# Last image of an attention layer: another order of its four head pairs, an output projection in two halves of the queries, and statistics read from the PSUM bank

## The chip, the cores and the metric

The kernel runs on one core of a Trainium2 chip. The metric is the device time of one execution in microseconds; the profile is of one execution, and its span lies a little under that execution's time.

## The reference

Four layers follow one another on x of shape 8 x 384 x 32 x 32, each added to its input. The change lies in the end of the first one, an attention over the 1024 pixels of each image with 8 heads of 48 channels:

```python
q = _dwproj(x, dw_q, g_q, b_q, pw_q).reshape(B, heads, hd, N)   # k and v alike
attn = softmax(einsum('bhcn,bhcm->bhnm', q, k) * scale)
out = einsum('bhnm,bhcm->bhcn', attn, v).reshape(B, C, H, W)
out = einsum('oc,bchw->bohw', w_out, out)
return _bn(out, g_out, b_out)      # mean and variance over all 8 images and all pixels
```

`_dwproj` is a depthwise 3x3 convolution, a batch normalisation, a GELU and a 384 x 384 projection. The second layer (a mixture of experts on the pixels, after a group normalisation of x plus this output) can't begin before the batch normalisation's statistics over all images are known. Layers three (a ternary convolution) and four (deformable attention) come after it.

## The kernel before

**Stages.** Stage A (until about 550 us) convolves all images and writes the raw results to memory. Stage B, where the change lies, is the attention, image after image (until about 1822 us). Then come `norms` (the batch normalisation's scale and shift, and the group statistics of what follows), a branch (L805) that recomputes the layer in a safer way if a softmax denominator was out of bounds, and the experts, which load their weights `w_sb` (L943) behind the branch.

**How stage B is tiled.** Channels lie on the 128 partitions, in KC = 3 blocks of 128; queries are cut into two halves of HALF = 512, keys into NT8 = 8 blocks of 128. The 8 heads are worked on as NPAIR0 = 4 pairs. Pairs 0, 1 and 2 carry 48 of each 64 rows of a block of projected queries and keys (`qk`); the rows that are left over in the three blocks make the two heads of pair 3. `gather_last` (L471, on SP's queue) copies them to `ql` as each block is projected. So pair 3 reads `ql` where the others read `qk`.

**Units and steps.** A unit is one pair with one half of the queries; it has four steps of NS = 2 key blocks. A step issues the scores (L638) of the step after it, the exponentials on ScalarE (L645), and then `weigh` (L653) of its own, which adds exp x values into two PSUM banks `pav`. At the second step of a unit (`kc == NS`) up to four entries of the list `todo` are issued as well: projections of the next pair (`project`, L572), projections of the output (`out_project`, L590), values. A scheduler keeps ScalarE in the order written and places the rest; TensorE runs its queue in order.

**`normalise`** (from L607) ends a unit on VectorE. It adds the two banks into `ta` (L610, L611), transposes blocks of 32 x 32 into `tu` (L614), where column HQ0 = 24 of each 32 holds the softmax denominator, takes its reciprocal into `rec` (L615), multiplies (L616) and transposes back. For pairs 0, 1 and 2 the result goes into channel block `pr` of `att` (L621). There 24 of each 32 rows are the pair's own and 8 belong to pair 3. For pair 3 it goes into `al` (L624), and `place_last` (L482) moves it as twelve strips of 8 rows x 512 (16 KB): strips 0 to 3 into block 0 of `att`, 4 to 7 into block 1, 8 to 11 into block 2. They are issued on SP, but for the very last unit alternately on SP and ScalarE's queue.

**`out_project`** multiplies `wo0` with the three blocks of `att` into a bank `po` (L590, three matmuls of 128x512). In the last image ScalarE copies the bank to `ot` (L601), VectorE takes `bn_stats` of `ot` (L602), ScalarE's queue stores `ot` (L603), and `cross` multiplies `ot` with the input half `xh` (L488; `xh` is loaded on SP, L587), sums it (L489) and aggregates (L141). `xh` and `ot` have two buffers each. `bank` takes from a pool of four PSUM banks that `pav` shares.

**End of the last image.** The units are in the order of pairs 0, 1, 2, 3. The output projection of queries 0 to 511 is queued in the second step of pair 3's second unit; that of queries 512 to 1023 follows the last unit. Then VectorE checks all of `rec` (L742, L743, L745), a matmul with ones (L747) and L748 make the flag `bad` of it, and `norms` begins: three aggregates over all images (L154), variance plus epsilon (L160), the power -0.5 on GpSimd (L95), the scale (L162) and a chain of small operations.

Of the kernel before, what the change touches and what calls it, by code (L numbers as in the profile page):

```python
# [9 lines left out]
ALU = mybir.AluOpType  # L10
AX = mybir.AxisListType

B, C, H, W = 8, 384, 32, 32
N = H * W
P = 128
KC = C // P
HALF = N // 2
# [8 lines left out]
NH0, HD0, NPAIR0 = 8, 48, 4  # L26
HQ0 = HD0 // 2
HS0 = 32 - HQ0
R_LO, R_HI = 1e-15, 1e15
# [23 lines left out]
def tile_kernel(ctx: ExitStack, tc: tile.TileContext, i: dict, out: bass.AP):  # L53
    nc = tc.nc
# [12 lines left out]
    def bank(name):  # L67
        return ps_mm.tile([P, HALF], F32, tag="mm", name=name)
# [148 lines left out]
    with ExitStack() as pa:  # L217
# [10 lines left out]
        for s in range(2):  # L228
            t = wa.tile([P, KC, H + 2, W], F32, name=f"pad{s}")
# [134 lines left out]
        for n, (b, g) in enumerate(work):  # L364
# [6 lines left out]
            if n in todo:  # L371
                f, b2 = todo.pop(n)
# [10 lines left out]
            for h, k in steps:  # L383
                dx, c0, c1, o0 = TAPS[k]
                rows = slice(h * (H // 2), (h + 1) * (H // 2))
                if g < NGC:
                    lhs, rhs = cw[:, g, dx, :], st[:, rows, c0:c1]
                else:
                    r = slice(32 * h, 32 * h + 3 * GR)
                    lhs, rhs = cwr[r, dx, :], st[r, rows, c0:c1]  # L390
                nc.tensor.matmul(  # L391
                    pk[h].rearrange("p (h w) -> p h w", w=W)[: 3 * nch, :, o0 : o0 + c1 - c0],
                    lhsT=lhs, rhs=rhs, start=(k == 0), stop=(k == 2),
                )
                if k == 2:
                    hs = slice(h * HALF, (h + 1) * HALF)
# [30 lines left out]
        for k, t in enumerate(two):  # L427
# [8 lines left out]
            start=True, stop=True,  # L436
# [3 lines left out]
            start=True, stop=True,  # L440
# [32 lines left out]
                in_=src[64 * j + HD0 : 64 * (j + 1), :],  # L473
            )

    def place_last(dst, src, queues):

        for k in range(12):
            j, d = divmod(8 * k, HD0)
            r = 64 * j + 32 * (d // HQ0) + d % HQ0  # L480
            q = 32 * (k % 4) + HQ0
            queues[k % len(queues)].dma_start(  # L482
                out=dst[q : q + HS0, k // 4, :], in_=src[r : r + HS0, :]
            )

    def cross(b, m, h, xh, ot):

        nc.vector.scalar_tensor_tensor(xh, xh, xmv[:, b, m, 0:1], ot, ALU.subtract, ALU.mult)  # L488
        nc.vector.reduce_sum(xo[:, b, m, h : h + 1], xh, AX.X)  # L489
        if h == 1:  # L490
            moments(omv[:, b, m, :], ost[:, m, 2 * b : 2 * b + 2, :])
# [11 lines left out]
    with ExitStack() as pb:  # L503
# [76 lines left out]
            if h == 1:  # L580
                gather_last(qks[b, KC, v], qks[b, pr, v], pr)

        def out_project(b, m, h):
            hs = slice(h * HALF, (h + 1) * HALF)
            xh = op.tile([P, HALF], F32, tag="xh", name=f"xh{b}_{m}_{h}")
            with tc.issue_after(w_last.ins) if b == 0 else nullcontext():
                nc.sync.dma_start(out=xh, in_=x_img[b][:, m, hs])  # L587
            po = bank(f"po{b}_{m}_{h}")
            for c in range(KC):
                nc.tensor.matmul(  # L590
                    po,
                    lhsT=wo0[:, c, m * P : (m + 1) * P],
                    rhs=atts[b][:, c, hs],
                    start=(c == 0),
                    stop=(c == KC - 1),
                )
            ot = op.tile([P, HALF], F32, tag="ot", name=f"ot{b}_{m}_{h}")
            if b + 1 < B:
                nc.vector.tensor_copy(ot, po)
            else:  # L600
                nc.scalar.copy(ot, po)  # L601
            nc.vector.bn_stats(ost[:, m, 2 * b + h, :], ot)  # L602
            (nc.sync if b + 1 < B else nc.scalar).dma_start(out=o_dram[b, :, m, hs], in_=ot)  # L603
            cross(b, m, h, xh, ot)

        def normalise(b, pr, h, pav):

            u = b * NU + pr * 2 + h
            ta = np_.tile([P, HALF], F32, tag="ta", name=f"ta{u}", bufs=1)
            nc.vector.tensor_copy(ta, pav[0])  # L610
            nc.vector.tensor_tensor(ta, pav[1], ta, ALU.add)  # L611
            tu = np_.tile([P, 16, 32], F32, tag="tu", name=f"tu{u}", bufs=1)
            tuf = tu.rearrange("p a b -> p (a b)")
            nc.vector.transpose(tuf, ta)  # L614
            nc.vector.reciprocal(rec[:, u, :], tu[:, :, HQ0])  # L615
            nc.vector.tensor_tensor(  # L616
                tu, tu, rec[:, u, :].unsqueeze(2).to_broadcast([P, 16, 32]), ALU.mult
            )
            hs = slice(h * HALF, (h + 1) * HALF)
            if pr < KC:  # L620
                nc.vector.transpose(atts[b][:, pr, hs], tuf)  # L621
            else:
                al = np_.tile([P, HALF], F32, tag="al", name=f"al{u}")
                nc.vector.transpose(al, tuf)  # L624
                last = b + 1 == B and h == 1
                place_last(
                    atts[b][:, :, hs], al, (nc.sync, nc.scalar) if last else (nc.sync,)
                )

        def scores(b, pr, h, kc):  # L630

# [16 lines left out]
        def weigh(b, pr, kc, pav, p):  # L648
            for k in range(2):
                r = slice(64 * k, 64 * k + 64)  # L650
                for j in range(2):
                    hd = 2 * pr + j
                    nc.tensor.matmul(  # L653
                        pav[k][64 * j : 64 * j + 64, :],
                        lhsT=vts[b % 2][r, kc, 2 * hd : 2 * hd + 2, :].rearrange(
                            "p a b -> p (a b)"
                        ),
                        rhs=p[r, j * HALF : (j + 1) * HALF],
                        start=(kc == 0),
                        stop=(kc == NT8 - 1),  # L660
                    )
# [4 lines left out]
        for v in range(2):  # L666
            for h in range(2):
                project(0, 0, v, h)

        NS = 2  # L670
        steps = [
            (b, pr, h, kc)
            for b in range(B) for pr in range(NPAIR0) for h in range(2)
            for kc in range(0, NT8, NS)
        ]
        todo = [lambda t=t: values(0, t) for t in range(NT8)]
# [8 lines left out]
        for n, (b, pr, h, kc) in enumerate(steps):  # L685
            if kc == 0:
                if pr == 0 and h == 0:
                    atts[b] = ap_.tile([P, KC, N], F32, tag="att", name=f"att{b}")
                    if b + 1 < B:
                        load_b(b + 1)  # L690
                    else:
                        for k in range(3):
                            fetch(k)
                if b == 0 and pr == 1 and h == 0:
                    values_tile(1)
                if b + 1 == B and pr == 2 and h == 0:
                    for k in range(3, 5):
                        fetch(k)
                if b + 1 == B and pr == 3 and h == 1:
                    todo += [lambda m=m: out_project(B - 1, m, 0) for m in range(KC)]  # L700
                if h == 0 and pr + 1 < KC:
                    todo += [
                        lambda v=v, q=q, b=b, pr=pr: project(b, pr + 1, v, q)
                        for v in (1, 0) for q in range(2)
                    ]
                if pr == 0 and h == 1 and b > 0:
                    todo += [
                        lambda m=m, q=q, b=b: out_project(b - 1, m, q)
                        for m in range(KC) for q in range(2)
                    ]  # L710
                if pr == 2 and h == 0 and b + 1 < B:
                    todo += [lambda t=t, b=b: values(b + 1, t) for t in range(NT8)]
                if pr == 3 and h == 0 and b + 1 < B:
                    todo += [
                        lambda v=v, q=q, b=b: project(b + 1, 0, v, q)
                        for v in (1, 0) for q in range(2)
                    ]
                pav = [bank(f"pav{b}_{pr}_{h}_{k}") for k in range(2)]
            cur = nxt
            if n + 1 < len(steps):  # L720
                nxt = scores_of(*steps[n + 1])
            if b + 1 < B:
                for v, c in GELUS.get(n % (len(steps) // B), ()):
                    gelu_chunk(acts[b + 1][2 - v], 2 - v, c)
            for k in range(NS):
                weigh(b, pr, kc + k, pav, cur[k])

            early = b == 0 and pr == 0 and h == 0
            if early or kc == NS:
                for _ in range(min(2 if early else 4, len(todo))):  # L730
                    todo.pop(0)()
            if kc == NT8 - NS:
                normalise(b, pr, h, pav)
        for t in todo:
            t()

        for m in range(KC):
            out_project(B - 1, m, 1)

        okt = pp.tile([P, B * NU * 16], F32, tag="p", name="okt")  # L740
        recf = rec.rearrange("p u q -> p (u q)")
        nc.vector.tensor_scalar(okt, recf, R_LO, None, ALU.is_ge)  # L742
        nc.vector.scalar_tensor_tensor(okt, recf, R_HI, okt, ALU.is_le, ALU.mult)  # L743
        okm = np_.tile([P, 1], F32, tag="okm", name="okm", bufs=1)
        nc.vector.tensor_reduce(okm, okt, AX.X, ALU.min)  # L745
# [59 lines left out]
    with tc.If(redo > 0):  # L805
        with ExitStack() as pb:
# [13 lines left out]
            with tc.For_i(0, B) as bi:  # L820
# [40 lines left out]
                for pr in range(NPAIR0):  # L861
                    qt, kt = qks[0][:, pr, :], qks[1][:, pr, :]
                    for h in range(2):
# [40 lines left out]
                                )  # L904
                        hs = slice(h * HALF, (h + 1) * HALF)
                        nc.vector.tensor_copy(att[:, pr, hs] if pr < KC else al[:, hs], pav)
                place_last(att, al, (nc.sync,))
                oe = work[4]
                for m in range(KC):
                    for h in range(2):  # L910
# [983 lines left out]
```

## Time and profile before

| | |
|---|---|
| median of 3 runs | 3751.69 us (3746.74 to 3756.45) |
| profiled execution, its own time | 3751.05 us |
| its span | 3749.3 us |
| mean granted TensorE clock | 0.981 |
| TensorE matmul busy | 3632.0 us (97%) |
| VectorE busy | 1820.6 us (49%) |
| ScalarE busy | 1280.2 us (34%) |
| a unit of the last image without projections | 13.75 us (1763.12 to 1776.87, `ta` to `ta`) |
| last weighing ends, branch is left | 1804.2 us, 1835.1 us |

A line of the timeline gives start, duration, engine, source line, operation, output <- input, count, and in brackets the idle time of the engine before it and what ended it. A float32 matmul has two records. "SPq" and "ACTq" are the queues that issue transfers, PE is TensorE, DVE VectorE, ACT ScalarE, POOL GpSimd. The table by windows has the window, its length, busy time and count of each engine, granted clock, share of the DMA engines and GB/s.

### The profile page before, as it was taken

What the parts mean: (1) busy time and instruction counts of PE and PEld (TensorE: products, weight loads), DVE (VectorE), ACT (ScalarE), POOL (GpSimd) and SP (SyncE); (2) the same over time, 40 slices, a digit from 0 to 9 for tenths busy, and PEclk for the clock granted to TensorE, in tenths of its full rate; (3) what the DMA queues carried; (4) which work ended last, traced back from release to release, by engine and by line L of the source; (5) the groups of instructions that cost most, each with busy time, mean ns of one, the idle gap of its engine ahead of it and who ended that gap; (6) DMA issues with size and microseconds to landing.
All of it is one profiled execution on the core that took longest, in us unless ns stands there. A gap on an engine that the chain in (4) does not pass through costs nothing.

```text
span 3749.3 us, 39325 instructions
## 1 busy us (share of the span) xinstructions
PE 3632.0 (97%) x15746; PEld 1533.0 (41%) x15746; DVE 1820.6 (49%) x2840; ACT 1280.2 (34%) x1536; POOL 199.5 (5%) x162
## 2 busy tenths in 40 slices
PE   7999999999999999999799999999999999999888
PEld 3444333333333333333244534444444444544433
DVE  6776223232323232333346557465663656547664
ACT  2222354545444454534112321323222232322222
POOL 0000100000000000000000010201001010010111
PEclk8999999999999999999899999999999999999898
DMA  6776311121212121211430000100001001010000
GB/s 198 232 251 229 131 54 36 62 63 37 63 40 75 26 72 28 71 43 55 183 140 34 17 34 17 40 28 17 34 17 51 17 17 40 19 43 17 0 34 18
DMA packets 83449, 242.49 MB, mean 65 GB/s; under 512 B 18563, under 2 KB 19091, under 8 KB 82873
## 3 DMA queue, kind: packets, MB, share of 16 engines
q1 hardware_dynamic: 70174, 200.42, 16.1%
q10 hardware_dynamic: 12504, 37.88, 3.0%
q8 instruction: 128, 2.10, 0.2%
q0 software_dynamic: 576, 1.55, 0.1%
q14 instruction: 67, 0.54, 0.0%
HBM read 122.64 MB, written 75.50 MB: 53 GB/s over the span
## 4 chain that ended last, share of the span: by engine, by line
PE 40%; DVE 9%; ACT 1%; issue 0%; DMA 0%; POOL 0%; DVEq 0%; POOLq 0%; ACTq 0%; SPq 0%
PE y L1281 11%; PE ph L1260 8%; DVE y L1355 6%; PE pq L1400 3%; PE pw L1363 3%; PE pf L1666 3%; PE s L1561 3%; PE pav L1577 2%; PE pss L1603 1%; DVE hd L1246 1%; DVE off L1470 1%; PE pk L1535 1%; PE pv L1544 1%; PE xsb L1521 1%; PE pom L1483 1%; PE plog L1023 0%
## 5 line engine op out<-in xcount | busy, mean ns | idle before, releaser
L645 ACT ACTIVATE p<-s 128x1024 f32<-128x1024 f32 x512 | 496.5, 1021 | 506.8 <-PE s L638 506.6
L1281 PE MATMUL y<-hd,w_sb 128*128 128x512 f32 x1080 | 490.2, 599 | 3.6 <-DVE hd L1246 3.6
L653 PE MATMUL pav<-p,vt 64*64 64x512 f32 x4096 | 487.0, 590 | 0.0
L1260 PE MATMUL ph<-h,w_sb 128*128 128x512 f32 x1104 | 483.3, 594 | 0.4 <-DMA w_sb<-in_w_dram 0.4
L638 PE MATMUL s<-qk,qk 48*64 48x512 f32 x3072 | 370.8, 597 | 3.3 <-ACT p L645 3.3
L391 PE MATMUL pk<-st,cw_sb 126*126 126x512 f32 x720 | 322.8, 610 | 9.5 <-DMA st<-pad 9.3
L1260 PEld LDWEIGHTS ph<-h,w_sb 128*128 128x128 f32 x1104 | 207.6, 190 | 253.5 <-issue 250.3
L1281 PEld LDWEIGHTS y<-hd,w_sb 128*128 128x128 f32 x1080 | 199.0, 191 | 249.3 <-issue 235.5
L653 PEld LDWEIGHTS pav<-p,vt 64*64 64x64 f32 x4096 | 156.6, 133 | 285.1 <-issue 285.1
L610 DVE COPY ta<-pav 128x512 f32<-128x512 f32 x64 | 44.2, 691 | 429.0 <-PE pav L653 425.9
L1355 DVE SCALAR_TENSOR_TENSOR y<-h,tap,y 128x992 f32<-128x992 f32 (+1 forms) x192 | 234.0, 1242 | 1.6
L391 PEld LDWEIGHTS pk<-st,cw_sb 126*126 126x126 f32 x720 | 140.4, 197 | 183.8 <-issue 179.1
L1470 DVE SCALAR_TENSOR_TENSOR off<-q,dw_sb,off 128x225 f32<-128x225 f32 (+3 forms) x432 | 213.1, 546 | 1.7
L1270 ACT ACTIVATE hd<-ph,b_sb 128x512 f32<-128x512 f32 x180 | 122.7, 681 | 258.6 <-PE ph L1260 258.3
L638 PEld LDWEIGHTS s<-qk,qk 48*64 48x64 f32 x3072 | 108.6, 133 | 231.1 <-issue 191.9
L78 DVE COPY qk<-pq 128x512 f32<-128x512 f32 x48 | 33.2, 691 | 292.7 <-PE pq L572 292.7
L397 ACT COPY y<-pk 126x512 f32<-126x512 f32 (+1 forms) x136 | 76.4, 583 | 255.2 <-PE pk L391 111.1
L1568 ACT ACTIVATE p<-s 128x1024 f32<-128x1024 f32 x96 | 93.1, 1021 | 173.0 <-PE s L1561 172.9
L590 PE MATMUL po<-att,wo_sb 128*128 128x512 f32 x288 | 132.8, 615 | 11.6 <-DMA att<-al 11.6
L1246 DVE TENSOR_TENSOR hd<-hd,cb 128x512 f32<-128x512 f32 x180 | 122.3, 684 | 35.5 <-ACT hd L1270 35.2
L1363 PE MATMUL pw<-y,upw 128*128 128x512 f32 x288 | 129.7, 603 | 7.6 <-DVE y L1355 7.6
L572 PE MATMUL pq<-g,wq_sb 128*128 128x512 f32 x288 | 131.2, 606 | 2.2 <-DMA wq_sb<-in_wq_dram 2.2
(280 smaller groups left out, 3961.2 us busy)
## 6 DMA issues: line engine op xcount, KB each, us to landing
g<-raw SPq DMA_DIRECT2D x72, 512.0 KB
st<-pad SPq DMA_DIRECT2D x180, 168.0 KB
raw<-y ACTq DMA_DIRECT2D x171, 168.0 KB
xa<-in_x_dram SPq DMA_DIRECT2D x24, 512.0 KB
xh<-in_x_dram SPq DMA_DIRECT2D x48, 256.0 KB
f<-in_x_dram SPq DMA_DIRECT2D x24, 512.0 KB
f<-o SPq DMA_DIRECT2D x24, 512.0 KB
o<-ot SPq DMA_DIRECT2D x42, 256.0 KB
```

The costliest lines, as they stand in the source:

```text
L391: nc.tensor.matmul(pk[h].rearrange("p (h w) -> p h w", w=W)[: 3 * nch, :, o0 : o0 + c1 - c0], lhsT=lhs, rhs=rhs, start=(k == 0), stop=(k = ...
L572: nc.tensor.matmul(pq, lhsT=w_in[v][:, c, pr * P : (pr + 1) * P], rhs=acts[b][v][:, c, h * HALF : (h + 1) * HALF], start=(c == 0), stop=(c ...
L590: nc.tensor.matmul(po, lhsT=wo0[:, c, m * P : (m + 1) * P], rhs=atts[b][:, c, hs], start=(c == 0), stop=(c == KC - 1),)
L638: nc.tensor.matmul(s[64 * k : 64 * k + 64, j * HALF : (j + 1) * HALF], lhsT=kt[r, k0 : k0 + 64], rhs=qt[r, h * HALF : (h + 1) * HALF], sta ...
L645: nc.scalar.activation(p, s, AF.Exp, scale=scale)
L653: nc.tensor.matmul(pav[k][64 * j : 64 * j + 64, :], lhsT=vts[b % 2][r, kc, 2 * hd : 2 * hd + 2, :].rearrange("p a b -> p (a b)"), rhs=p[r, ...
L1246: nc.vector.tensor_tensor(hd, hd, state["cb"], ALU.mult)
L1260: nc.tensor.matmul(ph, lhsT=w1[:, e, c, dc * P : (dc + 1) * P], rhs=state["h1"][c], start=(c == 0), stop=(c == KC - 1),)
L1281: nc.tensor.matmul(y, lhsT=w2[:, e, dc, m * P : (m + 1) * P], rhs=state[h, k], start=(k == 0), stop=(k == NE * KC - 1),)
L1355: nc.vector.scalar_tensor_tensor(d, f, tap2[:, c, t : t + 1], d, ALU.mult, ALU.add)
L1363: nc.tensor.matmul(pw[h], lhsT=upw2[:, c, m * P : (m + 1) * P], rhs=y[c][:, hs], start=(c == 0), stop=(c == KC - 1),)
L1470: nc.vector.scalar_tensor_tensor(d, f, dw3[:, t : t + 1], d, ALU.mult, ALU.add)
```

## The change

In the last image the order of the pairs is 0, 1, 3, 2. Pair 3's strips for channel blocks 0 and 1 of `att` go there as before, since those blocks are complete. Those for block 2 go to a spare place (`spare(0, h)`, in the values tile that the last image doesn't use), VectorE transposes that into `spare(1, h)`, and `normalise` of pair 2 writes its 24 of each 32 columns beside them there, so that one transpose writes the whole of block 2. All strips are issued on SP. `normalise` of the very last unit works by two halves of 256 queries, and so does the output projection behind it, into three banks that are taken beforehand. The statistics of that projection read the bank in place of `ot`. The check of `rec` is issued after the last transpose.

```diff
-    def place_last(dst, src, queues):
+    def place_last(dst, src, third=None):
         for k in range(12):
...
-            queues[k % len(queues)].dma_start(
-                out=dst[q : q + HS0, k // 4, :], in_=src[r : r + HS0, :]
-            )
+            to = dst[:, k // 4, :] if k < 8 or third is None else third
+            nc.sync.dma_start(out=to[q : q + HS0, :], in_=src[r : r + HS0, :])
...
-        def out_project(b, m, h):
+        def out_project(b, m, h, po=None):
...
-            po = bank(f"po{b}_{m}_{h}")
-            for c in range(KC):
+            po_new = po is None
+            if po_new:
+                po = bank(f"po{b}_{m}_{h}")
+            for c in range(KC if po_new else 0):
...
-            nc.vector.bn_stats(ost[:, m, 2 * b + h, :], ot)
+            nc.vector.bn_stats(ost[:, m, 2 * b + h, :], ot if po_new else po)
...
+        def spare(k, h):
+            vf = vts[B % 2].rearrange("p t h d -> p (t h d)")
+            return vf[:, (2 * k + h) * HALF : (2 * k + h + 1) * HALF]
...
         def normalise(b, pr, h, pav):
...
+            tv, tf = tu, tuf
+            if b + 1 == B and pr == 2:
+                tf = spare(1, h)
+                tv = tf.rearrange("p (a b) -> p a b", b=32)[:, :, :HQ0]
+            n = 2 if b + 1 == B and pr == 2 and h == 1 else 1
+            for k in range(n):
+                qs, qb = (slice(k * m // n, (k + 1) * m // n) for m in (HALF, 16))
+                nc.vector.tensor_copy(ta[:, qs], pav[0][:, qs])
+                nc.vector.tensor_tensor(ta[:, qs], pav[1][:, qs], ta[:, qs], ALU.add)
+                nc.vector.transpose(tuf[:, qs], ta[:, qs])
+                nc.vector.reciprocal(rec[:, u, qb], tu[:, qb, HQ0])
+                w = tv.shape[2]
+                nc.vector.tensor_tensor(
+                    tv[:, qb], tu[:, qb, :w],
+                    rec[:, u, qb].unsqueeze(2).to_broadcast([P, 16 // n, w]), ALU.mult,
+                )
+                dst = al if pr == KC else atts[b][:, pr, h * HALF : (h + 1) * HALF]
+                turned = nc.vector.transpose(dst[:, qs], tf[:, qs])
+            if pr == KC:
+                hs = slice(h * HALF, (h + 1) * HALF)
+                place_last(atts[b][:, :, hs], al, spare(0, h) if b + 1 == B else None)
+            return turned
...
+        ORDER = ((0, 1, 2, 3), (0, 1, 3, 2))
...
-            for b in range(B) for pr in range(NPAIR0) for h in range(2)
+            for b in range(B) for pr in ORDER[b + 1 == B] for h in range(2)
...
-                if b + 1 == B and pr == 2 and h == 0:
+                if b + 1 == B and pr == 3 and h == 0:
                     for k in range(3, 5):
                         fetch(k)
-                if b + 1 == B and pr == 3 and h == 1:
+                if b + 1 == B and pr == 2 and h == 1:
                     todo += [lambda m=m: out_project(B - 1, m, 0) for m in range(KC)]
...
+            if b + 1 == B and pr == 2 and h == 0 and kc == NS:
+                for k in range(2):
+                    nc.vector.transpose(spare(1, k), spare(0, k))
...
+        pos = [bank(f"po{B - 1}_{m}_1") for m in range(KC)]
+        for k in range(2):
+            qs = slice(k * HALF // 2, (k + 1) * HALF // 2)
+            for m in range(KC):
+                for c in range(KC):
+                    nc.tensor.matmul(
+                        pos[m][:, qs], lhsT=wo0[:, c, m * P : (m + 1) * P],
+                        rhs=atts[B - 1][:, c, HALF:][:, qs], start=(c == 0), stop=(c == KC - 1),
+                    )
         for m in range(KC):
-            out_project(B - 1, m, 1)
+            out_project(B - 1, m, 1, pos[m])
...
-        nc.vector.tensor_scalar(okt, recf, R_LO, None, ALU.is_ge)
+        with tc.issue_after(turned.ins):
+            nc.vector.tensor_scalar(okt, recf, R_LO, None, ALU.is_ge)
```

In the order that the scheduler builds of it, VectorE's queue has both `spare` transposes directly behind the transposes into `al`, and the two halves of the last `normalise` alternate operation by operation; TensorE's queue has the first half's channel blocks 0 and 1 for all three banks ahead of its block 2; the three L154 stand together, ahead of the last L488.

More of the change, by code (lines that the diff above doesn't have):

```diff
@@ L609, in normalise @@
             ta = np_.tile([P, HALF], F32, tag="ta", name=f"ta{u}", bufs=1)
-            nc.vector.tensor_copy(ta, pav[0])
-            nc.vector.tensor_tensor(ta, pav[1], ta, ALU.add)
             tu = np_.tile([P, 16, 32], F32, tag="tu", name=f"tu{u}", bufs=1)
             tuf = tu.rearrange("p a b -> p (a b)")
[L614 to L622, printed above, removed]
-                al = np_.tile([P, HALF], F32, tag="al", name=f"al{u}")
[L624 to L627, printed above, removed]
-                )
+            if pr == KC:
+                al = np_.tile([P, HALF], F32, tag="al", name=f"al{u}")
+            tv, tf = tu, tuf
[13 more added lines that the diff above has]
+                    rec[:, u, qb].unsqueeze(2).to_broadcast([P, 16 // n, w]), ALU.mult,
+                )
+                dst = al if pr == KC else atts[b][:, pr, h * HALF : (h + 1) * HALF]
+                turned = nc.vector.transpose(dst[:, qs], tf[:, qs])
+            if pr == KC:
+                hs = slice(h * HALF, (h + 1) * HALF)
+                place_last(atts[b][:, :, hs], al, spare(0, h) if b + 1 == B else None)
+            return turned
         def scores(b, pr, h, kc):
@@ L732, in tile_kernel @@
             if kc == NT8 - NS:
-                normalise(b, pr, h, pav)
+                turned = normalise(b, pr, h, pav)
         for t in todo:
             t()
+        pos = [bank(f"po{B - 1}_{m}_1") for m in range(KC)]
[7 more added lines that the diff above has]
+                    )
         for m in range(KC):
-            out_project(B - 1, m, 1)
+            out_project(B - 1, m, 1, pos[m])
         okt = pp.tile([P, B * NU * 16], F32, tag="p", name="okt")
         recf = rec.rearrange("p u q -> p (u q)")
-        nc.vector.tensor_scalar(okt, recf, R_LO, None, ALU.is_ge)
+        with tc.issue_after(turned.ins):
+            nc.vector.tensor_scalar(okt, recf, R_LO, None, ALU.is_ge)
         nc.vector.scalar_tensor_tensor(okt, recf, R_HI, okt, ALU.is_le, ALU.mult)
@@ L906, in tile_kernel @@
                         nc.vector.tensor_copy(att[:, pr, hs] if pr < KC else al[:, hs], pav)
-                place_last(att, al, (nc.sync,))
+                place_last(att, al)
                 oe = work[4]
```

## The prediction

> **What bounds the kernel now.** I read the page first: TensorE is busy 97% of the span, so the span shrinks mostly where TensorE stands still. Of the page's rows, one waits for something that the change edits, the output projection (L590):
>
> ```profile
> L590 PE MATMUL po<-att,wo_sb 128*128 128x512 f32 x288 | 132.8, 615 | 11.6 <-DMA att<-al 11.6
> ```
>
> All of its waiting, 11.6 us, is for the strips that `place_last` moves from `al` into `att`. Second view: TensorE's timeline over the end of the last image, whose last unit is pair 3, queries 512 to 1023.
>
> ```profile
> 1781.81 1.90 PE L653 MATMUL pav<-p,vt 64*64 64x512 f32 x16
> 1785.26 1.10 PE L590 MATMUL po<-att,wo_sb 128*128 128x512 f32 x2 [1.55 <-DMA att<-al]
> 1787.85 2.07 PE L590 MATMUL po<-att,wo_sb 128*128 128x512 f32 x2 [1.49 <-DMA att<-al]
> 1790.62 8.22 PE L590 MATMUL po<-att,wo_sb 128*128 128x512 f32 x14 [0.70 <-DMA att<-al]
> 1798.78 1.95 PE L638 MATMUL s<-ql,ql 48*64 48x512 f32 x16
> 1800.54 3.62 PE L653 MATMUL pav<-p,vt 64*64 64x512 f32 x32
> 1812.03 9.48 PE L590 MATMUL po<-att,wo_sb 128*128 128x512 f32 x18 [7.88 <-DMA att<-al]
> ```
>
> The four waits, 1.55, 1.49, 0.70 and 7.88, are the 11.6, so the whole of it lies here. Twelve strips leave SP's queue from 1780.89 on in 8.25 us, 0.69 each, and the middle projection's first three matmuls (two records each) start as the 4th, 8th and 12th land. From the weighing (L653) to the next scores takes 1798.78 - 1781.81 = 16.97 us. The table by windows shows that the granted clock (third column from the end) fell to half meanwhile:
>
> ```profile
> 1787.80:1790.60 2.80, 2.07 (x2) 0.51 (x3) 0.00 (x0) 0.00 (x0) 0.00 (x0) 0.50 0.11 21
> 1790.60:1793.00 2.40, 2.38 (x3) 1.17 (x4) 0.00 (x0) 0.30 (x1) 0.00 (x0) 0.50 0.00 0
> ```
>
> Then the timeline of all engines from the last weighing's end, 1804.2, to the branch:
>
> ```profile
> 1808.69 4.10 SPq L482 DMA_DIRECT2D att<-al  x6
> 1808.69 4.48 ACTq L482 DMA_DIRECT2D att<-al  x6
> 1809.80 1.22 DVE L745 TENSOR_REDUCE okm<-okt 128x1 f32<-128x1024 f32 x1
> ...
> 1821.55 0.58 ACT L601 COPY ot<-po 128x512 f32<-128x512 f32 x1 [1.99 <-PE po L590]
> ...
> 1825.67 0.16 DVE L162 TENSOR_TENSOR bnsc_out<-bnsc_out,gbo_sb 128x3 f32<-128x3 f32 x1 [0.82 <-POOL bnsc_out L95]
> ...
> 1835.12 0.35 SPq L943 DMA_DIRECT2D w_sb<-in_w_dram  x1
> ```
>
> From L162 on there is one chain (the norms, the branch at L805, the load of `w_sb`, the first `ph`), and all engines leave the branch together. So each microsecond gained before L162 is one of the span.
>
> **What the Trainium skill says.** "DMA: Bandwidth & Descriptors", section "Issuing engines are not separate DMA queues", holds that issuing from several engines saves only the sequencer's time, "usually small relative to the DMA itself". For these 16 KB strips the trace disagrees: their issue, 0.69 us each, is what spaces them. "TensorE: Matmul & The Clock Gate", section "What's actually happening", says that idleness halves the clock and that some 3.4 us of work restores it; the 0.50 above agrees. "PSUM — Partial Sum Buffer", section "PSUM bank collisions raise a hardware error", says that two engines reading one bank must be kept apart, ScalarE and VectorE included. No run shows that yet, but in the order of the changed program `bn_stats` on the bank waits for ScalarE's semaphore: it will follow the copy to `ot`, as now.
>
> **The change, part by part.** The sum is against the profiled execution's 3751.05 us (span 3749.3 and 1.75 around it), 0.64 under the median of 3751.69.
>
> 1. *Middle projection.* With pair 2 last, VectorE alone completes the third channel block of `att`, and the strips left two units earlier. In another unit two projections run unhindered, from a weighing at 1696.91 to L590 at 1698.74 (1.83) and on to the next block at 1703.99 (5.25 for six matmuls, 0.875 each). Nine take 7.88, with the 1.83 ahead 9.71. Gain 16.97 - 9.71 = **7.3 us**. This needs VectorE's last transpose in time. Its queue now holds the two `spare` transposes (0.71 each), and each waits for the last of twelve strips: 8.25 of issue and 1.5 to land (in the middle projection the last issue ends 1789.14, its matmul starts 1790.62). First: `al` done 1753.4, strips landed 1763.2, transpose until 1763.9, so the copy queued behind it starts 0.8 late. Second: `al` 1768.0, landed 1777.7, copy of pair 2 at 1778.5 instead of 1776.9, `att` done 1782.5. TensorE needs it for its third matmul, at 1785.4: 2.9 us spare, and VectorE idles 9.8 us in such a unit, so I cost both at nothing; no bank that TensorE wants next is held. The `xh` loads, now behind 24 strips on SP, are released after 1788, when that queue has been empty for over 10 us. The multiply's 24 columns instead of 32 save some 0.14 us (691 ns at 512, 418 at 256), hidden likewise.
>
> 2. *Pair 3 moved forward.* Its queries come by `gather_last`, whose last two copies (L471, on SP's timeline, behind a 512 KB load) now have 1.4 us before they are needed, where they had 29:
>
> ```profile
> 1728.59 0.33 SPq L169 DMA_DIRECT2D f<-in_x_dram  x1
> 1729.42 1.15 SPq L471 DMA_DIRECT2D ql<-qk  x2
> ```
>
> The scores that start at 1731.98 become pair 3's. In the DMA view each transfer ends in packets under 512 B; the 48 of that load and of both copies are over by 1732.7, and a strip's wait ended 0.4 after its last such packet. So the weights of the second head load near 1733.1 instead of 1731.7, the first head's somewhat earlier: **1.3 us lost**, since all else on TensorE is queued behind. The trace shows no such wait; bounds: 0 (landed in time) to 4 (2.3 until two more loads have crossed it, and half of 3.4 us at half clock, an estimate from the clock page).
>
> 3. *Tail*, with the last weighing's end held at 1804.2. VectorE's order interleaves the two halves. 128x256 operations take 0.42 (rows of that shape: 418 ns) and follow one another after 0.34 where independent; copies, adds, transposes, reciprocals (0.25) and multiplies by twos put the first half's `att` at 3.4 us, 1807.6, the second's at 1808.0, and the checks after it (L742 to L745: 0.68, 1.18, 1.22) end at 1811.0, as now. TensorE meanwhile does channel blocks 0 and 1 of the first half: 128x256 records follow at 0.216 (L1535: 17 in 3.64), 0.43 a matmul, six until 1806.6; three more from 1807.7 to 1809.0; the second half's nine complete the banks at 1810.2, 1811.5 and 1812.8, against 1816.4, 1819.0 and 1821.55. The strips' 4.48 is gone from that path and from ScalarE's queue. Now VectorE is the bound: from 1811.05 three `bn_stats` (0.61), two L488 (0.65), two L489 (0.63), three L141 (0.12) and the flag make 4.8; three L154 (0.45) until 1817.2, the last L488, then L160 at 1817.9 and L162 at 1819.0 (1.12 behind, as now). The last `xh`, issued at 1813.7 after the first L489, takes about 2.9 (now 1819.5 to 1822.4): 0.6 to spare. Gain 1825.67 - 1819.0 = 6.7, less 0.1 for `xs_c`, which now stands in that chain: **6.5 us**. Bounds: 4.5 (`xh` late by 1, the copies to `ot` and reads of PSUM 1 more) to 8 (VectorE's steps overlapped better).
>
> Sum: 7.3 + 6.5 - 1.3 = **12.5 us**, 0.33%.
>
> **The rivals.**
> - *A smaller gain*: the gather's wait is 4 and the tail 4.5, so 7.3 + 4.5 - 4 = 7.8, near 3744. For it: the fetches fill the DMA engines (303 GB/s from 1732 to 1735). Against: the copies' packets were over before those of the two later loads.
> - *A larger gain*: gather in time and tail 8, 15.3 in all, 3736. For it: the tail's steps are costed one after another. Against: the packet times.
> - *The change doesn't do what it says*: statistics from the bank begin no sooner. Already in the sum, and no loss against now.
> - *Slower*: VectorE's queue stands at the `spare` transposes. With t per strip `att` is ready at 1753.4 + 2(12t + 2.2) + 8.1, so TensorE waits once t is over 0.81 us, 24 us longer for each one of t. At t = 1.33 that eats the 12.5; at the longest strip issue of the trace, 1.54, the kernel is 5 slower: 3757. For it: that issue occurred. Against: the median is 0.62, and the DMA share is 0.02 from 1735 to 1783.
>
> **How the numbers follow.** A measurement of this kernel can tell about 0.3% (11.3 us; its three runs lie 9.7 apart). Chances: forecast 0.70, larger gain 0.13, smaller 0.11, slower 0.06. The forecast's 12.5 is 1.2 over that bound, with 2.5 of doubt either way, so 0.7 of its chance counts as faster: 0.49 + 0.13 = 0.62; same 0.21 + 0.11 = 0.32; slower 0.06. Time: 3751.7 - 12.5 = 3739.2. The range spans the larger and the smaller gain, 3736 to 3744, and the 2 to 3 us that a median of such runs moves: 3733 to 3746.
>
> **What would show it.** In the changed profile: no wait for `att<-al` on TensorE; from weighing to scores around the middle projection near 9.7 us, at clock 1.00; a new wait on `ql<-qk` of about 1.3 ahead of pair 3's first scores; 14.9 us from the last weighing's end to L162's counterpart (now 21.5), VectorE unbroken over its second half. It is wrong if TensorE waits for VectorE's `att` at the middle projection, if the `ql` wait comes with a clock of 0.50, or if the last bank's product waits for `xh`.

## The result, and the profile after

The changed kernel's median is 3741.04 us (8 runs, 3739.02 to 3744.77) against 3751.99 us for the kernel before (8 runs, 3746.74 to 3756.45). The ratio is 0.997, with a 95% interval of 0.9959 to 0.9981. That is 10.95 us or 0.29% less, between 7.1 and 15.4 us by the interval. It lies just under the 0.3% that the prediction took as the bound of what such a measurement can tell; the interval leaves out a ratio of 1, and reaches to both sides of 0.3%. The forecast of 3739.2 us was 1.8 us too low. The profiled execution took 3740.91 us, with a span of 3739.1 us (before: 3749.3) and a mean granted clock of 0.982.

In this kernel L591 is the output projection by 512 queries (before: L590) and L764 the one by halves of 256. The matmuls of scores are L654, of weighing L669. First the groups by line, each shape apart (busy time, mean ns of one | idle time before, and what ended it):

```profile
L591 PE MATMUL po<-att,wo_sb 128*128 128x512 f32 x270 | 119.9, 598 | 0.0
...
L764 PE MATMUL po<-att,wo_sb 128*128 128x256 f32 x36 | 8.3, 385 | 0.5 <-DVE att L640 0.5
```

The 11.6 us of waiting for `att<-al` are gone entirely; what is left is 0.5 us, for VectorE's own transpose. TensorE's timeline over the same stretch as in the prediction shows where they went, and the price in its first line:

```profile
1733.20 2.06 PE L654 MATMUL s<-ql,ql 48*64 48x512 f32 x16 [0.98 <-DMA ql<-qk]
...
1783.05 2.04 PE L669 MATMUL pav<-p,vt 64*64 64x512 f32 x16
1785.02 7.99 PE L591 MATMUL po<-att,wo_sb 128*128 128x512 f32 x18
1792.94 1.95 PE L654 MATMUL s<-qk,qk 48*64 48x512 f32 x16
1794.71 3.62 PE L669 MATMUL pav<-p,vt 64*64 64x512 f32 x32
1798.25 2.86 PE L764 MATMUL po<-att,wo_sb 128*128 128x256 f32 x12
1801.61 5.45 PE L764 MATMUL po<-att,wo_sb 128*128 128x256 f32 x24 [0.50 <-DVE att L640]
```

The middle projection's 18 records follow one another without a gap. From its weighing to the next scores it takes 1792.94 - 1783.05 = 9.89 us, against 16.97. The table by windows (granted clock third from the end) shows no fall to half any more:

```profile
1783.00:1787.00 4.00, 4.00 (x25) 1.90 (x18) 0.00 (x0) 1.55 (x2) 0.00 (x0) 1.00 0.01 2
1787.00:1793.00 6.00, 6.00 (x19) 2.37 (x18) 3.91 (x6) 1.17 (x2) 0.00 (x0) 1.00 0.31 98
```

VectorE's timeline from the last weighing's end on; L777 is the last of the checks (before: L745), L603 is `bn_stats`, L487 the product with `xh` (before: L488):

```profile
1798.36 0.76 DVE L630 COPY ta<-pav 128x256 f32<-128x256 f32 x2 [2.62 <-PE pav L669]
...
1801.12 0.76 DVE L640 STREAM_TRANSPOSE att<-vt 128x256 f32<-128x256 f32 x2
...
1803.75 1.22 DVE L777 TENSOR_REDUCE okm<-okt 128x1 f32<-128x1024 f32 x1
1805.12 0.70 DVE L603 BATCH_NORM_STATS2 ost<-po 128x6 f32<-128x512 f32 x1 [0.15 <-ACT ot L602]
...
1809.72 1.47 DVE L154 BATCH_NORM_AGGREGATE bnmv_out<-ost 128x2 f32<-128x96 f32 x3
1811.11 0.68 DVE L487 SCALAR_TENSOR_TENSOR xh<-xh,xmv,ot 128x512 f32<-128x512 f32 x1
1811.71 0.16 DVE L160 TENSOR_SCALAR bnsh_out<-bnmv_out 128x3 f32<-128x3 f32 x1
...
1812.84 0.16 DVE L162 TENSOR_TENSOR bnsc_out<-bnsc_out,gbo_sb 128x3 f32<-128x3 f32 x1 [0.33 <-POOL bnsc_out L95]
```

From the copy into `ta` to L162 it is 1812.84 - 1798.36 = 14.48 us, against 21.48. VectorE has one idle stretch in it, 0.15 us, before GpSimd's step.

**Where the gain went.** The start of an execution scatters: the first scores behind the last query projection came between 1724.4 and 1732.9 us, and not by kernel. So I measure from there, in five stretches that end with the load of `w_sb` behind the branch, and add the time from that load to the first `ph`, the experts' matmul that reads it. The "middle weighing" is the last one ahead of the middle projection. The three rows of the kernel before and the two of the changed one are separate executions; the others are the experiments below. All in us, as differences of starts in the timelines.

| kernel | first scores to middle weighing | to the next scores | to `ta` | `ta` to L162 | to `w_sb` | sum | `w_sb` to first `ph` |
|---|---|---|---|---|---|---|---|
| before | 53.32 | 16.97 | 5.41 | 21.48 | 9.45 | 106.63 | 9.06 |
| before_again | 53.33 | 16.88 | 5.41 | 21.51 | 9.44 | 106.57 | 8.82 |
| before_again2 | 53.32 | 17.03 | 5.42 | 21.59 | 9.46 | 106.82 | 9.06 |
| after | 54.50 | 9.89 | 5.42 | 14.48 | 9.35 | 93.64 | 10.91 |
| after_again | 54.60 | 9.89 | 5.42 | 14.47 | 9.40 | 93.78 | 10.71 |
| order_only | 54.67 | 9.89 | 5.42 | 14.56 | 9.50 | 94.04 | 9.82 |
| stats_ot | 54.42 | 9.90 | 5.42 | 15.80 | 9.38 | 94.92 | 10.84 |
| gather_first | 53.32 | 10.22 | 5.42 | 14.48 | 9.57 | 93.01 | 10.81 |
| sums_act | 53.32 | 10.24 | 5.42 | 13.46 | 9.44 | 91.88 | 9.10 |
| strips24 | 54.68 | 20.62 | 5.42 | 14.48 | 9.52 | 104.72 | 10.47 |

The stretch that the change edits is 106.67 - 93.71 = 12.96 us shorter (means of three and of two). Behind the branch, up to the first `ph`, 10.81 - 8.98 = 1.8 us of it are given back. That leaves 11.1. The medians' 10.95 agrees with it, but their interval, 7.1 to 15.4, holds 12.96 as well: the traces show this loss, the medians don't. Nor does it last to the end in every execution. From the load of `w_sb` to the end of the span the three executions of before take 1914.2 to 1914.3 us, the changed kernel 1916.9 (after) and 1913.4 (after_again), and all seven kernels with the new order 1913.4 to 1917.7, on average 1915.8.

### The profile page after: what moved, and what is told of

Its sections match the earlier page's. It is cut to its first block, busy times and chain, and to the rows that moved or that the text cites. A ratio compares the mean times of both kernels' runs of the same rounds, so it can differ in the third digit from the quotient of the medians.

```text
span 3739.1 us, 39371 instructions
## 1 busy us (share of the span) xinstructions
PE 3631.8 (97%) x15764; PEld 1552.9 (42%) x15764; DVE 1822.2 (49%) x2848; ACT 1281.0 (34%) x1536; POOL 199.5 (5%) x162
## 4 chain that ended last, share of the span: by engine, by line
PE 40%; DVE 9%; ACT 1%; issue 0%; DMA 0%; POOL 0%; DVEq 0%; POOLq 0%; ACTq 0%; SPq 0%
PE y L1313 11%; PE ph L1292 8%; DVE y L1387 6%; PE pq L1432 3%; PE pw L1395 3%; PE pf L1698 3%; PE s L1593 3%; PE pav L1609 2%; PE pss L1635 1%; DVE hd L1278 1%; DVE off L1502 1%; PE pk L1567 1%; PE pv L1576 1%; PE xsb L1553 1%; PE pom L1515 1%; PE plog L1055 0%
## 5 line engine op out<-in xcount | busy, mean ns | idle before, releaser
L669 PE MATMUL pav<-p,vt 64*64 64x512 f32 x4096 | 489.0, 590 | 0.0
L1292 PE MATMUL ph<-h,w_sb 128*128 128x512 f32 x1104 | 483.3, 594 | 0.8 <-DMA w_sb<-in_w_dram 0.8
L654 PE MATMUL s<-qk,qk 48*64 48x512 f32 x3072 | 371.7, 597 | 3.3 <-ACT p L661 3.3
L1292 PEld LDWEIGHTS ph<-h,w_sb 128*128 128x128 f32 x1104 | 207.6, 190 | 253.9 <-issue 252.0
L669 PEld LDWEIGHTS pav<-p,vt 64*64 64x64 f32 x4096 | 164.5, 133 | 277.1 <-issue 268.9
L630 DVE COPY ta<-pav 128x512 f32<-128x512 f32 (+1 forms) x65 | 44.3, 682 | 410.6 <-PE pav L669 410.6
L654 PEld LDWEIGHTS s<-qk,qk 48*64 48x64 f32 x3072 | 112.2, 133 | 227.7 <-issue 184.7
L1624 POOL TENSOR_TENSOR p<-p,p 128x1024 f32<-128x1024 f32 x48 | 112.9, 2353 | 350.6 <-ACT p L1600 326.3
```

Of the source, the lines that this page charges most:

```text
L654: nc.tensor.matmul(s[64 * k : 64 * k + 64, j * HALF : (j + 1) * HALF], lhsT=kt[r, k0 : k0 + 64], rhs=qt[r, h * HALF : (h + 1) * HALF], sta ...
L669: nc.tensor.matmul(pav[k][64 * j : 64 * j + 64, :], lhsT=vts[b % 2][r, kc, 2 * hd : 2 * hd + 2, :].rearrange("p a b -> p (a b)"), rhs=p[r, ...
L1292: nc.tensor.matmul(ph, lhsT=w1[:, e, c, dc * P : (dc + 1) * P], rhs=state["h1"][c], start=(c == 0), stop=(c == KC - 1),)
```

## The experiments

**Two more executions of the kernel before, and one set of the changed one.** No edit.

> The kernel before once more, for a second profile of what follows the branch. In its first profile the w_sb load was there 9.0 us after its issue; in four profiles with the new order it took 9.8 to 10.9. Theory (chance): it takes more than 9.5 here too, and the rest of the span after w_sb's issue lies in the 1913 to 1918 us of the others. Rival (the new order makes the load slower): 9.0 again.

> As before_again, a third profile of the kernel before: chance says that the w_sb load's time scatters as in the kernels with the new order, between 9 and 11 us; the rival says 9.0 a third time.

> The changed kernel once more, for a second profile. In the first one the branch is left 12.9 us earlier than before, but the span is only 10.2 shorter. Theory (chance: where the clock's windows fall, and how fast the w_sb load lands): from w_sb's issue to the first ph it is somewhere between 8.9 and 11 us, not again 10.9, and the rest of the span varies by 1 to 2 us. Rival (the change makes the load or the restart slower): 10.9 and the same later losses again, span 3739 again.

The two single executions of before took 3746.97 and 3753.78 us; after_again has a median of 3739.93 us (6 runs, 3734.11 to 3747.04), ratio 0.9973 (0.9961 to 0.9985). What is edited repeats within 0.3 us, as the table shows, while whole times scatter by 7 to 13 us. Of the 6.8 us between before_again and before_again2, 6.5 lie ahead of the first scores; of the 6.8 between after and after_again, 3.4 lie there and 3.5 behind the load of `w_sb`.

The theory of chance fails in before_again: it asked for more than 9.5 us from the load to the first `ph`, and 8.82 came. The 9.06 of before_again2 is the rival's 9.0. In after_again neither side came true whole: 10.71 us is close to the rival's 10.9, but the later losses did not come again, and the span was 3732.3 us, not 3739. L1023 and L1055 are the experts' first matmuls behind the branch, L1260 and L1292 the first that read `w_sb`. TensorE's timeline, first before_again:

```profile
1832.10 7.58 PE L1023 MATMUL plog<-f,gate 128*32 128x512 f32 x52 [6.92 <-DVE gate L1007]
1839.80 10.54 PE L1260 MATMUL ph<-h,w_sb 128*128 128x512 f32 x24
```

And after_again:

```profile
1820.08 8.70 PE L1055 MATMUL plog<-f,gate 128*32 128x512 f32 x52 [6.95 <-DVE gate L1039]
1829.61 10.54 PE L1292 MATMUL ph<-h,w_sb 128*128 128x512 f32 x24 [0.82 <-DMA w_sb<-in_w_dram]
```

`plog` takes 8.70 instead of 7.58 us, and `ph` then still waits 0.82 us for the weights (0.40 in before, 0.33 in before_again2). Two things are late. The granted clock behind the branch stays at 0.50 for longer: reckoned by proportion from windows of 1 us, for some 2.8 us of `plog` in before_again and 5.1 in after_again (2.7 in before and 5.5 in after). And `w_sb` lands later: 10.7 us after its issue, where in before_again it had landed by 8.8. By 7 us after the issue some 2.3 MB have moved in both, which is nearly the whole load; from there to the start of `ph` it took 1.8 us in the one and 3.7 in the other. What causes either isn't settled. gather_first has the short clock (`plog` 7.54 us) and the late weights (a wait of 2.09 us); sums_act has neither much. In all three executions of before this stretch takes at most 9.06 us, in all seven of kernels with the new order more, by 0.04 to 1.85. That the branch comes earlier doesn't explain it: strips24 (below) issues the load at 1835.41 us, before did at 1835.12, and strips24 takes 10.47.

**order_only: the order of pairs alone.** Pair 2 last, the `spare` transposes, all strips on SP and the later check of `rec` stay; the last unit and its projection are whole, and the statistics read `ot` again.

```diff
-            n = 2 if b + 1 == B and pr == 2 and h == 1 else 1
+            n = 1
...
-        pos = [bank(f"po{B - 1}_{m}_1") for m in range(KC)]
-        for k in range(2):
...
         for m in range(KC):
-            out_project(B - 1, m, 1, pos[m])
+            out_project(B - 1, m, 1)
```

> The order of pairs and the spare transposes alone: the last unit's normalise whole, its projection by 512 queries, statistics from ot. Theory (order and removed strips carry the gain, halves and statistics next to nothing): middle projection 9.9 us from weighing to scores as in the changed kernel (17.0 before); VectorE whole needs 3.9 us to the last transpose instead of 3.4, but the checks behind it end at 7.0 after the last weighing instead of 6.6 and VectorE is the bound from there, so L162 comes 14.7 to 14.9 us after the last weighing's end (14.5 changed, 21.5 before); in all 0.2 to 0.4 us above the changed kernel, so some 10.5 us under the kernel before. Rival (the halves make the tail): L162 at 17 or later, gain under 9 us.

Median 3739.33 us (5 runs, 3735.65 to 3740.95), ratio to before 0.9965 (0.9952 to 0.9979), not to be told from the whole change. The timelines of TensorE and of VectorE:

```profile
1781.23 2.04 PE L669 MATMUL pav<-p,vt 64*64 64x512 f32 x16
...
1791.12 1.95 PE L654 MATMUL s<-qk,qk 48*64 48x512 f32 x16
...
1800.45 4.56 PE L591 MATMUL po<-att,wo_sb 128*128 128x512 f32 x10 [0.32 <-DVE att L640]
```

```profile
1796.54 0.69 DVE L630 COPY ta<-pav 128x512 f32<-128x512 f32 x1 [2.63 <-PE pav L669]
...
1802.27 1.22 DVE L768 TENSOR_REDUCE okm<-okt 128x1 f32<-128x1024 f32 x1
1803.41 0.68 DVE L603 BATCH_NORM_STATS2 ost<-ot 128x6 f32<-128x512 f32 x1
...
1811.10 0.16 DVE L162 TENSOR_TENSOR bnsc_out<-bnsc_out,gbo_sb 128x3 f32<-128x3 f32 x1 [0.33 <-POOL bnsc_out L95]
```

The middle takes 9.89 us, and `ta` to L162 14.56 us, 0.08 more than in the changed kernel and a little under the 14.7 to 14.9 expected. VectorE goes from the check (L768) straight into `bn_stats`, without the 0.15 us of waiting: ScalarE's copy of the first bank starts at 1801.62, while the check still runs. So the tail is VectorE's own work, whether the projection comes in halves or whole, and **the new order, with what it needs, carries the whole gain**. "What it needs" is the `spare` place and all strips on SP; the later check came along too, and what it is worth by itself was not run.

**stats_ot: all of the change but the statistics.**

```diff
-            nc.vector.bn_stats(ost[:, m, 2 * b + h, :], ot if po_new else po)
+            nc.vector.bn_stats(ost[:, m, 2 * b + h, :], ot)
```

> The changed kernel with bn_stats of the last three banks on ot again. Theory (the bank's statistics wait for ScalarE's copy anyway): bn_stats start where they start in the changed kernel, 0.62 after each copy's start; the scheduler places the three L154 differently, so L160 may move by 0.5 either way, but no more. Rival (reading the bank starts the statistics earlier): each bn_stats 0.6 us later than in the changed kernel, L162 at 15 or later.

One execution, 3740.33 us. VectorE's timeline:

```profile
1804.30 0.69 DVE L603 BATCH_NORM_STATS2 ost<-ot 128x6 f32<-128x512 f32 x1 [0.15 <-ACT ot L602]
...
1809.89 0.75 DVE L487 SCALAR_TENSOR_TENSOR xh<-xh,xmv,ot 128x512 f32<-128x512 f32 x1 [0.48 <-DMA xh<-in_x_dram]
...
1811.05 0.63 DVE L488 TENSOR_REDUCE xo<-xh 128x1 f32<-128x512 f32 x1
...
1812.20 0.17 DVE L160 TENSOR_SCALAR bnsh_out<-bnmv_out 128x3 f32<-128x3 f32 x1
1813.34 0.16 DVE L162 TENSOR_TENSOR bnsc_out<-bnsc_out,gbo_sb 128x3 f32<-128x3 f32 x1 [0.97 <-POOL bnsc_out L95]
```

The first `bn_stats` waits for the copy to `ot` and starts 6.76 us behind `ta` (1797.54), exactly as in the changed kernel: reading the bank makes no read earlier. Yet L162 comes 15.80 us behind `ta`, 1.3 us later, and L160 with it: more than the 0.5 that the theory allowed, and as late as the rival said, though not for the rival's reason. The scheduler placed the work differently: here the last sum (L488) and `xs_c` (a small operation on all the sums, L806) stand ahead of L160, where the changed kernel lets L488 run while GpSimd is at its step, and the last product waits 0.48 us for `xh`. So beside the halves this edit is worth 1.3 us, in one execution, through the order that the scheduler builds of it; with neither edit, order_only is as quick as the kernel with both. The statistics from the bank with a whole last unit were not run.

**gather_first: the fetches behind the gather.** The two fetches of the last image's experts' input, which the change puts at pair 3, are issued after the last gather of the queries.

```diff
+                        with tc.issue_after(gathered[b, 2, 0].ins):
+                            fetch(k)
```

> The changed kernel with the two fetches of the last image's middle issued behind the last gather of pair 3's queries. Theory (the gather's wait is made by the 512 KB load issued ahead of it): the wait on ql falls from 1.0 us to under 0.5, scores of pair 3 start within 0.6 us of the place where they were free, 0.6 to 1.1 us gained on the changed kernel. Rival (issue and landing of the two copies alone make the wait): issue still starts after VectorE's copy at 1729.4 and ends 1.15 later, with 1.5 to land the wait stays at 0.7 to 1.0 and the gain is under 0.3.

Median 3739.79 us (5 runs, 3735.75 to 3743.26), ratio 0.9964 (0.9951 to 0.9978). The timeline of TensorE and of SP's queue (L169 is a fetch, L471 the gather):

```profile
1731.76 1.14 SPq L471 DMA_DIRECT2D ql<-qk  x2
1732.60 1.90 PE L671 MATMUL pav<-p,vt 64*64 64x512 f32 x16
1733.00 1.48 SPq L169 DMA_DIRECT2D f<-o  x3
1734.32 1.94 PE L656 MATMUL s<-ql,ql 48*64 48x512 f32 x14
```

Pair 3's first scores follow 1.72 us behind the weighing, as everywhere else; the wait is gone, as the theory had it. The gather is issued where it was, 0.93 us behind the first scores (1729.48 in the changed kernel), and other loads follow at once here too. What differs in front of it is the one load of 512 KB at 1728.65 that the prediction shows; both fetches moved, and that load was not moved by itself. Of the 1.2 us gained in the table's first stretch 0.3 come back in the second, where this program has one scores matmul behind the first weighing matmul of a step, and 0.2 between L162 and `w_sb`. The path is 0.7 us shorter, too little for the medians to show.

**strips24: the spare transposes late.** In the last image each strip is cut into two of 4 rows, so that 24 issues of half the size move the same bytes.

```diff
+            for e in range(0, HS0, 4) if third is not None else (None,):
+                w = slice(0, HS0) if e is None else slice(e, e + 4)
...
+                    out=to[q : q + HS0, :][w, :], in_=src[r : r + HS0, :][w, :]
```

> The changed kernel with the last image's strips cut into two of 4 rows, 24 issues a unit instead of 12. Theory (the spare transposes stand in VectorE's queue until the last strip lands, and the margin is about 3 us): issue of a unit's strips takes 16.5 us, the copy of pair 2 starts some 16 to 17 us late, its banks are freed so late that TensorE waits 12 to 13 us for them at the middle projection, clock halves for a while: 12 to 16 us slower than the changed kernel, about as slow as before or up to 5 slower. Rival (the strips are hidden whatever they take): no wait at the middle projection, time of the changed kernel.

Median 3749.78 us (12 runs, 3745.8 to 3755.37), ratio to before 0.9997 (0.9988 to 1.0006): the whole gain is gone. That is 8.7 us slower than the changed kernel, where 12 to 16 were expected. Timelines of SP's queue, VectorE and TensorE:

```profile
1756.97 10.10 SPq L485 DMA_DIRECT2D att<-al  x16
1767.18 4.99 SPq L485 DMA_DIRECT2D vt<-al  x8
...
1788.22 4.99 SPq L485 DMA_DIRECT2D vt<-al  x8
```

```profile
1773.54 0.71 DVE L751 STREAM_TRANSPOSE vt<-vt 128x512 f32<-128x512 f32 x1 [16.59 <-DMA vt<-al]
...
1794.52 0.71 DVE L751 STREAM_TRANSPOSE vt<-vt 128x512 f32<-128x512 f32 x1 [16.39 <-DMA vt<-al]
...
1798.27 0.71 DVE L644 STREAM_TRANSPOSE att<-vt 128x512 f32<-128x512 f32 x1
```

```profile
1785.37 2.04 PE L673 MATMUL pav<-p,vt 64*64 64x512 f32 x16
1795.87 10.20 PE L595 MATMUL po<-att,wo_sb 128*128 128x512 f32 x18 [8.46 <-DVE ta L634]
1805.99 1.52 PE L658 MATMUL s<-qk,qk 48*64 48x512 f32 x12
```

The chain that the fourth rival described is all there. 24 issues take 15.1 us, where 16.5 were expected; the first transpose ends late and holds pair 3's second unit on VectorE, the second holds pair 2's first, and `att` is done at 1798.98. The rival's formula, with 15.1 for 12t and with this run's first `al` done at 1756.95, gives 1756.95 + 2 (15.1 + 2.2) + 8.1 = 1799.7. TensorE stands still for 8.46 us, and then runs in part at half clock (10.20 us instead of 7.99). In all the middle takes 10.7 us longer (20.62 against 9.89). By the rival's other figure, 24 us for each one of t over 0.81, a t of 15.1 / 12 = 1.26 makes 10.8. It is not `att` that TensorE waits for first, but a PSUM bank: `pav`, held until VectorE's copy into `ta` (L634). In the changed kernel itself the same queues are in time, SP's first and then VectorE's:

```profile
1754.65 5.38 SPq L483 DMA_DIRECT2D att<-al  x8
1760.14 2.63 SPq L483 DMA_DIRECT2D vt<-al  x4
```

```profile
1764.25 0.71 DVE L747 STREAM_TRANSPOSE vt<-vt 128x512 f32<-128x512 f32 x1 [9.62 <-DMA vt<-al]
...
1778.21 0.71 DVE L747 STREAM_TRANSPOSE vt<-vt 128x512 f32<-128x512 f32 x1 [9.37 <-DMA vt<-al]
...
1781.95 0.71 DVE L640 STREAM_TRANSPOSE att<-vt 128x512 f32<-128x512 f32 x1
```

**sums_act: three sums on ScalarE.** On top of gather_first, the last three sums of `xh` run on ScalarE behind its copies, and the last `xh` has a place of its own, so that its load doesn't wait.

```diff
+        if act:
+            sums.append((xh, xo[:, b, m, h : h + 1]))
+        else:
+            nc.vector.reduce_sum(xo[:, b, m, h : h + 1], xh, AX.X)
...
+            if po is None or m < 2:
...
+                xh = spare(2, 0)
...
+        for xh, to in sums:
+            nc.scalar.activation(xh, xh, AF.Identity, accum_out=to)
```

> gather_first, and the last three sums over pixels (L489) taken from VectorE to ScalarE behind its three copies, the last bank's xh in the values tile that is free (so that its load needs no buffer). Theory (VectorE bounds the tail from the first bn_stats on): two sums of 0.63 leave the path ahead of L160, which comes 12.4 us after the last weighing's end instead of 13.3, L162 at 13.5 instead of 14.5; 1.0 us gained in the tail and 1.2 at the gather, 2 in all against the changed kernel, some 13 against before. Rival (banks and copies bound the tail): L162 stays at 14.5.

Median 3738.94 us (5 runs, 3734.76 to 3741.21), ratio 0.996 (0.9946 to 0.9974). `ta` (1801.85) to L162 is 13.46 us, 1.0 less than in the changed kernel, as VectorE's timeline has it:

```profile
1814.17 0.17 DVE L160 TENSOR_SCALAR bnsh_out<-bnmv_out 128x3 f32<-128x3 f32 x1
1815.31 0.16 DVE L162 TENSOR_TENSOR bnsc_out<-bnsc_out,gbo_sb 128x3 f32<-128x3 f32 x1 [0.97 <-POOL bnsc_out L95]
```

Taking two sums (0.67 us each) off VectorE ahead of L160 moves L160 by 1.03 us, as the theory had it: VectorE is what bounds the tail. (The last load of `xh` came earlier as well; in the changed kernel nothing waited for it.) The path to `w_sb` is the shortest of all, 91.88 us. Its median is the lowest too, but its interval and those of order_only and gather_first overlap.

## Why the prediction came out nearly right

*Middle projection*, 7.3 predicted: measured 16.96 - 9.89 = **7.1 us**, at clock 1.00. The copy, the two `spare` transposes and the multiply cost nothing, as costed: `att` was done at 1782.66 (1781.95 + 0.71), 4.1 us ahead of the third matmul (some 1786.8, two times 0.88 behind the first at 1785.02), where 2.9 was estimated. strips24 shows what this slack protects.

*Gather*, -1.3 predicted between 0 and 4: measured **-1.2 us**, with 0.98 of it shown as idle, and no fall of the clock. The reading by the DMA packets was good to 0.1 to 0.2 us, and gather_first shows that a load ahead of the gather made it late.

*Tail*, 6.5 predicted: measured **7.05 us** (21.53 - 14.48). Step by step from `ta`: TensorE starts on `att`'s first half at 3.25 us (1801.61; the half was predicted for 3.4), the first `bn_stats` at 6.76 (6.85), L160 at 13.35 (13.7), L162 at 14.48 (14.9). The three terms that were too large are small ones: the checks ended a little earlier, VectorE's steps overlapped more than their sum says (6.59 us from the first `bn_stats` to L160, 6.85 predicted), and `xs_c` cost nothing, since it ran behind L162. The last `xh` was issued at 1807.77; in stats_ot one landed 3.1 us after its issue, so here it came some 0.2 us ahead of its use at 1811.11, less than the 0.6 estimated.

The sum of the three is 12.9 us, against 12.5. The weak step is an earlier one: "each microsecond gained before L162 is one of the span". From L162 to the load of `w_sb` it holds (9.35 to 9.57 us, 9.45 before); behind the branch 1.8 us were lost up to the first `ph`, in a stretch that the forecast put at no difference without looking at it. 12.5 predicted, 0.4 more gained, 1.8 lost make 11.1. That this comes within 0.2 us of the medians is in part luck: their interval is 8 us wide, and from the load of `w_sb` to the end the changed kernel's two executions lie 2.7 us above and 0.8 us under the kernel before.

Of the rivals, *the change doesn't do what it says* came true for the statistics: they begin no sooner, in the changed kernel as in stats_ot after a wait of 0.15 us for the copy to `ot`. The prediction had this in its sum. It was silent on how little the halves do: its tail named the halves' `att` and the banks done early, and then VectorE as the bound, without drawing from it that the projection might stay whole; order_only shows that it might. The *smaller* and the *larger gain* rested on a gather that was late by 4 or by nothing and a tail of 4.5 or 8; neither came. The *slower* one had the right mechanism and a condition that this program doesn't meet: 12 strips took 8.1 us (5.38 and 2.63 with a gap of 0.1), 0.68 for each, under its 0.81. What it missed is the bank that TensorE wants before it wants `att`; the expectation of strips24 had it.

## What to carry to other kernels

If the last piece of work needs a slow rearrangement by DMA behind it, put another piece last and let one engine finish the data where they are: here the order of four pairs alone brought what it brought together with the halves, the banks taken beforehand and the statistics. When a step is moved forward, look at what stands ahead of its loads in their queue; the 1.2 us here vanished when the fetches were issued behind the gather. And a gain ahead of a branch and a large load is a gain of the whole only if the restart behind it is unchanged (here it took 0.0 to 1.9 us more, cause open), so read that stretch too.

## What the runs showed of the hardware that I had not expected

- Halving a strip hardly shortens its issue: 0.68 us for 16 KB (8 in 5.38), 0.63 for 8 KB (16 in 10.10). Between these two sizes it was the number of issues that set the time. The Trainium skill's "DMA: Bandwidth & Descriptors" calls the sequencer's share "usually small relative to the DMA itself" in "Issuing engines are not separate DMA queues"; for these strips it is not: twelve take 8.1 us to issue, and the transpose that waits for the last one starts 1.4 to 1.5 us after that issue ends.
- Behind the branch TensorE ran at half clock for 2.7 to 5.5 us of unbroken `plog`, in different executions of much the same work. The 3.4 us that the Trainium skill's "TensorE: Matmul & The Clock Gate" gives in "What's actually happening" lie inside that range. The page says itself that its window runs freely, and puts the scatter of the change at 0.5 us either way; here it is larger.
- Of a load of 2304 KB nearly all had moved 7 us after its issue, yet the matmul that waited for it could start only 2.1 us (before) to 3.9 us (after) later.
